# Rank products laid out in sequence, the norm's root ahead of the rank copy, and zero fills issued in steps

## The chip, the cores and the metric

The kernel runs on one core of one Trainium2 chip. The core has five engines with an instruction queue each: PE (TensorE, matmuls; its weight loads are listed as PEld), DVE (VectorE), ACT (ScalarE), POOL (GpSimd) and SP (SyncE, which here only issues DMAs). DMA engines move data between the device's main memory and the on-chip buffer. The metric is the device time of one execution, in microseconds (us). Times of before and after are medians over several executions. Profiles come from one profiled execution.

## The reference

The computation is a chain of four rounds over a graph with 3125 nodes of 256 features and 50000 edges, sorted by destination. Each round is a graph layer and a feed-forward layer with experts, both behind a layer norm and added to the nodes' features:

```python
x = x + _L0_gnn_ref(_layernorm(x), edge_weight, src, dst)      # segment_sum(w * xn[dst]) into src
x = x + _L0_ffn_ref(_layernorm(x)[None], ...)[0]               # top-2 of 8 experts
x = x + _L1_gnn_ref(_layernorm(x), edge_index, ...)            # attention, 4 heads, twice
x = x + _L1_ffn_ref(...)[0]
x = x + _L2_gnn_ref(...) ; x = x + _L2_ffn_ref(...)[0]
x = x + _L3_gnn_ref(...) ; x = x + _L3_ffn_ref(...)[0]
```

The change touches only the set-up (in which the edges are put in order on the chip) and the first graph layer, `_L0_gnn_ref`: for each edge, the normed features of one end, times the edge's weight, are added to the features of the other end.

## The kernel before

**Tiles.** The 3125 nodes lie in T = 25 blocks of P = 128 (one node per partition), each node with D = 256 features. `X` holds all nodes. The edges lie in 416 columns of 128 slots: 17 columns (KB) for each of the first 24 destination blocks, 8 (KL) for the last.

**Set-up, `look`.** It sorts and bins the edges. Near its end, `own_send(21)` issues 21 indirect DMAs from POOL (L1881), which scatter records of another graph into `os_table`. Beside them run two generators. `norm_sums` computes mean and variance of the nodes on ACT (L1338, L1343), and in its last step scales the sums (L1345), takes the root (`rsqrt`, L168, on ACT with a load of its function table; then five small DVE operations, L170 to L174) and L1347. `rank_edges` finds the rank of each edge among those of one source block:

- L1418 (DVE) makes `h`, a 0/1 mark of shape (edge column, source block) in bf16, `P x 416 x 25`, in three cuts of 204, 204 and 8 columns. L1424 (PE) counts with it.
- L1432 (DVE) fills `eqd`, 16 planes of 416 columns with equality marks. L1437 (PE) adds them with an identity matrix: 16 matmuls of 416 columns.
- L1443 (DVE) multiplies `h` with the starts of each block into `q`, again `P x 416 x 25`, cut by cut. L1448 (PE) adds the 25 unit products: matmul t reads `q[:, :, t]`, one element in 25.
- L1451 (ACT) copies the sum, the ranks, out of PE's accumulation buffer. After it stands `next(norm)`, the root.

In `look`, the instructions of DVE and of ACT keep the order in which the program writes them. Then a flag (L1329, L1330, DVE) tells whether the edges fit; `settle` (L1893) issues one DMA from SP; all engines read the flag (L2848) and branch. The rest of the work stands in `FAST_STEPS`.

**The fills, `clear`.** It is the first of these steps: 26 DMAs from SP, 1 MB each, that write zeros into `regions` (27 MB in main memory). `regions` is scattered into at the end of round one's graph layer (L872) and read by the feed-forward layer.

**Round one's graph layer, `r0_gnn`.** It first fills buckets for five destination blocks (`fill_bucket`, L1500). A bucket needs ACT for one-hot rows of ranks (L1515, L1516, 17 columns), DVE for L1519, L1523 and L1530, PE for 17 matmuls (L1526), and ACT for two copies (L1528, L1529). Then it runs through five groups g of five destination blocks, and in each through 25 source blocks: 125 steps. One step is:

- DVE compares for the source (L1600, `r_hs`) and the destination (L1605, `r_hd`, five times);
- PE multiplies them into five 128 x 128 weight blocks (L1609, `r_pw`);
- ACT copies these out (L1613, `r_wt`) into one fifth of a `wide` buffer, of which there are two; when a buffer is full, SP writes its 1.6 MB to `mats` (L1615);
- PE applies the blocks of the step before to the normed features (L1575, `r_pa`), DVE adds the result into `X` (L1576), ACT copies a column (L1577); POOL issues two sends.

While group g runs, the buckets of group g + 1 are filled, one in five steps. In the last group each step also scatters a block into `regions`. Outside `look` a scheduler sets the order of the instructions on each engine from its own estimates of durations, and an engine works in that order; SP's queue is one of them. A DMA holds one of eight semaphores ("lanes") shared by SP's and ACT's queues; the next DMA on the lane can be issued only when the one before has landed. ACT's queue also issues small loads (`gx_b`, L965) and three 1 MB zero writes (`ff_results`, L1015) during g = 0.

Of the kernel before, what the change touches and what calls it, by code (L numbers as in the profile page):

```python
# [25 lines left out]
BF16 = mybir.dt.bfloat16  # L26
# [7 lines left out]
P = 128  # L34
N = 3125
T = 25
# [15 lines left out]
KB = 17  # L52
# [11 lines left out]
class Net:  # L64
# [30 lines left out]

    def clear(self):

        v = self.regions.rearrange("(q p r) d -> q p r d", p=P, r=8)
        for q in range(v.shape[0]):
            self.nc.sync.dma_start(v[q], self.zero[:, None, 0:D].to_broadcast([P, 8, D]))  # L100

# [1114 lines left out]
class Fast(Net):  # L1218
# [171 lines left out]
    def rank_edges(self, pool, eqd, identb, both, over, norm):  # L1390


        nc, tc, s = self.nc, self.tc, self.d
        K = s.K
        with tc.tile_pool(name="re_ps", bufs=2, space=PSUM) as psp, tc.tile_pool(name="re_pr", bufs=1, space=PSUM) as psr:
            blk = pool.tile([P, K], BF16, name="re_blk")
            bi = pool.tile([P, K], I32, name="re_bi")
            nc.vector.tensor_copy(bi, s.rec[:, :, 0])
            nc.vector.tensor_scalar(bi, bi, 7, None, op0=OP.arith_shift_right)
            base = pool.tile([P, K], F32, name="re_base")  # L1400
            self.block_start(base)

            far = pool.tile([P, K], F32, name="re_far")

            place = s.rec[:, :, 1]
            nc.vector.tensor_sub(place, place, base)
            nc.vector.tensor_scalar(far, place, float(P), 64.0, op0=OP.is_ge, op1=OP.mult)
            nc.vector.tensor_tensor(blk, bi, far, OP.add)
            h = pool.tile([P, K, T], BF16, name="re_h")
            start = pool.tile([P, T, T], BF16, name="re_start")  # L1410
            top = pool.tile([P, 3], F32, name="re_top")
            cuts = ((0, 12, KB), (12, T - 1, KB), (T - 1, T, KL))
            sums = []
            last = psr.tile([P, 512], F32, name="re_r")
            for i, (u, v, kb) in enumerate(cuts):
                n = (v - u) * T
                k0, k1 = s.k0[u], s.k0[u] + (v - u) * kb
                nc.vector.tensor_tensor(h[:, k0:k1], blk[:, k0:k1, None].to_broadcast([P, k1 - k0, T]),  # L1418
                                        self.iotab[:, None, 0:T].to_broadcast([P, k1 - k0, T]), OP.is_equal)
                hv = h[:, k0:k1, :].rearrange("p (d k) s -> p k d s", k=kb)  # L1420
                ps = psp.tile([P, 2, 512], F32, name="re_p") if i < 2 else last[:, K:K + 2 * T].rearrange("p (j s) -> p j s", j=2)
                for j in range(2):
                    for k in range(kb):
                        nc.tensor.matmul(ps[:, j, 0:n].rearrange("p (d s) -> p d s", s=T), both[:, j, :], hv[:, k],  # L1424
                                         start=k == 0, stop=k == kb - 1)
                sums.append(ps)
            next(norm)

            for ks, ds, nd, kb in self.parts():
                bv = blk[:, ks].rearrange("p (d k) -> p d k", k=kb)  # L1430
                for g in range(1, kb):
                    nc.vector.tensor_tensor(eqd[:, g - 1, ks].rearrange("p (d k) -> p d k", k=kb)[:, :, g:kb],  # L1432
                                            bv[:, :, g:kb], bv[:, :, 0:kb - g], OP.is_equal)
            q = pool.tile([P, K, T], BF16, name="re_q")
            ranks = last[:, 0:K]
            for g in range(1, KB):
                nc.tensor.matmul(ranks, identb, eqd[:, g - 1, :], start=g == 1, stop=False)  # L1437
            for i, (u, v, kb) in enumerate(cuts):
                n = (v - u) * T
                k0, k1 = s.k0[u], s.k0[u] + (v - u) * kb  # L1440
                nc.vector.tensor_copy(start[:, u:v, :].rearrange("p d s -> p (d s)"), sums[i][:, 0, 0:n])
                four = [P, v - u, kb, T]
                nc.vector.tensor_tensor(q[:, k0:k1, :].rearrange("p (d k) s -> p d k s", k=kb),  # L1443
                                        h[:, k0:k1, :].rearrange("p (d k) s -> p d k s", k=kb),
                                        start[:, u:v, None, :].to_broadcast(four), OP.mult)
                nc.vector.tensor_reduce(top[:, i:i + 1], sums[i][:, 1, 0:n], AX.X, OP.max)
            for t in range(T):
                nc.tensor.matmul(ranks, identb, q[:, :, t], start=False, stop=t == T - 1)  # L1448
            nc.vector.tensor_reduce(over, top, AX.X, OP.max)
            nc.vector.tensor_scalar_add(over, over, float(-P))  # L1450
            nc.scalar.copy(s.rank, ranks)  # L1451
            next(norm)

    def block_start(self, base):

# [76 lines left out]
    def r0_gnn(self):  # L1532
# [5 lines left out]
        nc, tc, s = self.nc, self.tc, self.d  # L1538
# [3 lines left out]
        G = 5  # L1542
        self.mix_way = ExitStack()
        m = self.mix = self.mix_start(self.mix_way, "L0_ffn_Wg", ("L0_ffn_bg", "L0_ffn_bias"), 8, act=True)
        with ExitStack() as ctx:
            pool = ctx.enter_context(tc.tile_pool(name="r0", bufs=1))
# [12 lines left out]
            def norm(t):  # L1559
                nc.scalar.activation(xn[:, t, 0:D], self.X[:, t, :], AF.Identity, scale=s.rstd[:, t:t + 1],  # L1560
                                     bias=s.mean[:, t:t + 1])
# [10 lines left out]
            def apply(g, src, wt):  # L1572
                pa = psa.tile([P, D + 1], F32, name="r0_pa")
                for i in range(G):
                    nc.tensor.matmul(pa, wt[:, i, :], xn[:, g * G + i, :], start=i == 0, stop=i == G - 1)  # L1575
                nc.vector.tensor_add(self.X[:, src, :], self.X[:, src, :], pa[:, 0:D])  # L1576
                nc.scalar.copy(degs[:, src, g:g + 1], pa[:, D:D + 1])  # L1577
                if g == T // G - 1:

                    self.mix_send(m, 2)  # L1580
                    for _ in range(1 if src < T - 2 else 2):
                        self.mix_step(m, src + 1)


            for d in range(G):
                for _ in self.fill_bucket((bp, psb), f5, d):
                    pass
                self.own_send(8, self.filled)
            last = None
            for g in range(T // G):  # L1590
                ds = slice(g * G, g * G + G)
                for src in range(T):
                    if g == 0 and src + TG < T:
                        norm(src + TG)
                    if g + 1 < T // G:
                        if src % G == 0:
                            fill = self.fill_bucket((bp, psb), f5, (g + 1) * G + src // G)
                        next(fill, None)
                    hs = hp.tile([P, G, P], F32, name="r0_hs")
                    nc.vector.tensor_tensor(hs, self.iota[:, None, :].to_broadcast([P, G, P]),  # L1600
                                            s.bsrc[:, ds, src, None].to_broadcast([P, G, P]), OP.is_equal)
                    hd = hp.tile([P, G, P], F32, name="r0_hd")
                    for i in range(G):
                        d = g * G + i
                        nc.vector.tensor_scalar(hd[:, i, :], iota1, s.bdst[:, d, src:src + 1], s.bw[:, d, src:src + 1],  # L1605
                                                op0=OP.is_equal, op1=OP.mult)
                    pw = psw.tile([P, G, P], F32, name="r0_pw")
                    for i in range(G):
                        nc.tensor.matmul(pw[:, i, :], hd[:, i, :], hs[:, i, :], start=True, stop=True)  # L1609
                    if src % G == 0:  # L1610
                        wide = wp.tile([P, G, G, P], F32, name="r0_wt")
                    wt = wide[:, src % G]
                    done = nc.scalar.copy(wt, pw)  # L1613
                    if src % G == G - 1:
                        nc.sync.dma_start(self.mats[:, src - G + 1:src + 1, ds, :], wide)  # L1615
                    if last:
                        apply(*last)
                    last = (g, src, wt)
                    self.own_send(2 if g < T // G - 1 else src % 2, done)
# [1215 lines left out]
        self.own_graph.close()  # L2835


FAST_STEPS = ("clear", "r0_gnn", "take_edges", "middle", "r2_gnn", "r2_ffn", "r3_gnn", "r3_ffn")
STEPS = ("clear", "sort_src", "sort_dst", "r0_gnn", "r0_ffn", "r1_gnn", "r1_ffn", "sort_own", "r2_gnn", "r2_ffn",
         "r3_gnn", "r3_ffn")  # L2840

# [2 lines left out]
def network(ctx: ExitStack, tc: tile.TileContext, a, out):  # L2844
# [4 lines left out]
    for fast in (True, False):  # L2849
        with cmp.Else() if not fast else tc.If(fits > 0) as cmp, ExitStack() as way:  # L2850
            way_net = object.__new__(Fast if fast else Net)
            way_net.__dict__.update(net.__dict__, way=way, fast=fast)
            way_net.edges = way.enter_context(tc.tile_pool(name="edges", bufs=1))
            for step in FAST_STEPS if fast else STEPS:
                getattr(way_net, step)()
# [32 lines left out]
```

## Time and profile before

| what | value |
|---|---|
| median of 6 runs | 5660.24 us (5647.51 to 5676.73) |
| the profiled execution | 5653.63 us, span 5651.7 us |
| busy share of the span | PE 65%, DVE 49%, ACT 39%, POOL 37% |
| set-up until the flag (L1330) | 135.8 us |
| the 26 zero fills, first to last issue | 136.50 to 246.8 us |
| `r_wt` copy of step 0 and of step 24 of g = 0 | 172.33 and 324.01 us |
| the same of steps 0 and 24 of g = 1 | 327.35 and 410.28 us (3.46 a step) |

The times in the profile count from the start of the span. In a timeline a row has the start, the time, the engine, the source line, the operation with its output and inputs, the size, and how many instructions were joined into the row; in brackets stands how long the engine had been idle and what ended that: another engine's instruction, a DMA, or "issue" where the profile shows nothing that was waited for. A table by stretches has the busy time of each engine, the clock that PE was granted as a share of its full one, the busy share of the DMA engines and the rate that they moved. A list of waits has total, number and longest.

### The profile page before, as it was taken

The page shows a single profiled execution, that of the slowest core. Times are in us where ns is not written, and L with a number is a line of the kernel's source. Part 1 is how long each engine was busy: PE and PEld are TensorE (multiplying, and loading weights), DVE is VectorE, ACT ScalarE, POOL GpSimd, SP SyncE. Part 2 cuts the span into 40 slices and gives each one's busy share as a digit, 9 for nine tenths or more (in the row PEclk, how much of TensorE's full clock was granted, in tenths as well). Part 3 has the DMA queues.
Part 4 walks back from the last instruction along what each step waited for, and adds up shares of the span by engine and source line. Part 5 has one row for each costly group of instructions (what it writes and reads, how often), then busy time and mean ns, then how long its engine had stood idle before and what let it go on. Part 6 is the DMA issues. An engine that isn't in the chain of part 4 may idle for free. (4 is left out here: it accounts for less than half of the span.)

```text
span 5651.7 us, 66370 instructions
## 1 busy us (share of the span) xinstructions
PE 3678.1 (65%) x21000; PEld 2882.9 (51%) x21000; DVE 2793.5 (49%) x9308; ACT 2189.7 (39%) x6055; POOL 2107.0 (37%) x2108
## 2 busy tenths in 40 slices
PE   5499879335554324444573887554666699997994
PEld 2499768223333223333352776432333488886883
DVE  7588631534444334554525787425545788422112
ACT  4656422135454335455411897311222443112221
POOL 3566333555555455565357000245554000011003
PEclk8699979666666656666696998776777899997997
DMA  1632256333333133333162321201111011233554
GB/s 56 216 109 94 103 165 212 108 88 105 96 106 96 52 86 103 90 103 96 59 199 76 110 101 71 58 18 26 22 22 25 8 58 65 88 102 131 188 189 142
DMA packets 329539, 542.62 MB, mean 96 GB/s; under 512 B 69426, under 2 KB 242102, under 8 KB 325972
## 3 DMA queue, kind: packets, MB, share of 16 engines
q1 hardware_dynamic: 213520, 354.48, 18.7%
q0 software_dynamic: 84032, 154.27, 10.5%
q10 hardware_dynamic: 31620, 29.44, 1.6%
q8 instruction: 174, 2.85, 0.2%
q14 instruction: 193, 1.58, 0.1%
HBM read 393.09 MB, written 145.37 MB: 95 GB/s over the span
## 5 line engine op out<-in xcount | busy, mean ns | idle before, releaser
L363 POOL DMA_INDIRECT ad_rows<-r_rows,fa_gi x832 | 829.5, 997 | 621.4 <-PE ad_acc L2278 333.8
L1881 POOL DMA_INDIRECT os_table<-os_rec,os_at x512 | 544.4, 1063 | 642.8 <-ACT gx_h L1008 183.5
L363 POOL DMA_INDIRECT ad_rows<-q_rows,own_gi x416 | 400.6, 963 | 869.2 <-DVE ad_hb L2159 508.4
L2268 ACT ACTIVATE ad_rows<-ad_rows 128x64 f32<-128x64 f32 x2544 | 637.1, 335 | 121.3 <-issue 119.3
L2278 PE MATMUL ad_acc<-ad_rows,ad_hd 128*128 128x260 f32 x1664 | 596.4, 519 | 37.2 <-ACT ad_rows L2268 32.8
L2278 PEld LDWEIGHTS ad_acc<-ad_rows,ad_hd 128*128 128x128 f32 x1664 | 413.9, 263 | 126.6 <-ACT ad_rows L2268 42.2
L1710 PE MATMUL r_pa<-r_xs,r_cnt 128*128 128x257 bf16 (+1 forms) x3750 | 459.0, 276 | 11.6 <-issue 10.7
L872 POOL DMA_INDIRECT regions<-gh_xn,gd_at x150 | 148.4, 989 | 843.5 <-PE r_pa L1710 544.8
L1008 ACT ACTIVATE gx_h<-gx_pa,gx_bias 128x256 f32<-128x256 f32 x392 | 184.7, 473 | 605.9 <-PE gx_pa L1007 558.3
L1710 PEld LDWEIGHTS <-r_cnt 128*128 128x128 bf16 x3750 | 364.4, 99 | 66.2 <-issue 15.2
L1007 PE MATMUL gx_pa<-gx_xt,gx_w 128*128 128x256 f32 x1568 | 370.3, 392 | 23.7 <-DVE gx_xt L1002 21.8
L977 PE MATMUL gx_po<-gx_w,gx_h 128*128 128x256 f32 x1568 | 373.0, 384 | 9.5 <-ACT gx_h L1008 8.1
L979 DVE TENSOR_TENSOR gx_ys<-gx_po,gx_b 128x256 f32<-128x256 f32 x168 | 70.6, 423 | 567.5 <-PE gx_po L977 505.2
L1007 PEld LDWEIGHTS gx_pa<-gx_xt,gx_w 128*128 128x128 f32 x1568 | 297.6, 194 | 90.8 <-DVE gx_xt L1002 40.8
L363 POOL DMA_INDIRECT gb_y<-ff_results,gd_at x150 | 154.4, 1029 | 487.2 <-SPq L126 437.2
L1575 PE MATMUL r_pa<-r_xn,r_wt 128*128 128x257 f32 x1250 | 306.9, 391 | 35.0 <-ACT r_wt L1613 32.6
L2167 ACT CAST ad_hd<-ad_hb 128x2176 f32<-128x2176 bf16 (+1 forms) x50 | 98.3, 1967 | 581.6 <-PE ad_acc L2278 430.7
L2181 PE MATMUL ad_pt<-ident,ad_e 128*4 128x128 f32 x75 | 26.1, 348 | 452.4 <-DVE ad_e L2178 184.4
L977 PEld LDWEIGHTS gx_po<-gx_w,gx_h 128*128 128x128 f32 x1568 | 293.8, 193 | 51.7 <-ACT gx_h L1008 12.1
L2655 PE MATMUL ss_sum<-r_xw,ss_wt 128*128 128x256 f32 x1250 | 289.9, 394 | 6.3 <-DMA ss_wt<-mats 6.3
L2237 PE MATMUL ad_px<-ad_nb,ad_hT 128*128 128x24 bf16 x1248 | 45.4, 180 | 341.6 <-DVE ad_nb L1470 235.9
L1575 PEld LDWEIGHTS r_pa<-r_xn,r_wt 128*128 128x128 f32 x1250 | 233.3, 196 | 67.0 <-ACT r_wt L1613 34.4
(588 smaller groups left out, 7230.7 us busy)
## 6 DMA issues: line engine op xcount, KB each, us to landing
gx_w<-in_L_ffn_W SPq DMA_DIRECT2D x56, 1024.0 KB
mats<-r_wt SPq DMA_DIRECT2D x25, 1600.0 KB
ss_wt<-mats SPq DMA_DIRECT2D x25, 1600.0 KB
gx_w<-in_L_ffn_W SPq DMA_DIRECT2D x56, 512.0 KB
regions<-zero SPq DMA_DIRECT2D x26, 1024.0 KB
ad_rb<-fa_relT SPq DMA_DIRECT2D x48, 544.0 KB
gx_xs<-regions SPq DMA_DIRECT2D x84, 256.0 KB
ff_results<-gx_ys ACTq DMA_DIRECT2D x84, 256.0 KB
```

What stands on the lines that cost most here:

```text
L363: return self.nc.gpsimd.indirect_dma_start(out=out, out_offset=None, in_=table[:, :], in_offset=bass.IndirectOffsetOnAxis(ap=idx, axis=0))
L872: ins = nc.gpsimd.indirect_dma_start(out=self.regions[:, :], out_offset=bass.IndirectOffsetOnAxis(ap=m.at[i][:, t:t + 1], axis=0), in_=x, ...
L977: nc.tensor.matmul(po, h[:, f, j * P:(j + 1) * P], w2s[:, f, :], start=f == 0, stop=f == FC - 1)
L1007: nc.tensor.matmul(ps, w1s[:, c, f * P:(f + 1) * P], xt[:, c, :], start=c == 0, stop=c == DC - 1)
L1008: done = nc.scalar.activation(h[:, f, :], ps, act, bias=bias1[:, f, k:k + 1])
L1575: nc.tensor.matmul(pa, wt[:, i, :], xn[:, g * G + i, :], start=i == 0, stop=i == G - 1)
L1710: nc.tensor.matmul(pa[:, 0:n], c[:, u, :], xs[i][:, u, j, 0:n], start=u == 0 and j == 0, stop=u == T - 1 and j == 2)
L1881: i = nc.gpsimd.indirect_dma_start(out=s.table[:, :], out_offset=bass.IndirectOffsetOnAxis(ap=s.at[:, c:c + 1], axis=0), in_=s.rec[:, c, : ...
L2167: nc.scalar.copy(x.hd[:, :x.kb, :], x.hb[:, :x.kb, :])
L2268: i = nc.scalar.activation(v, v, AF.Copy, scale=x.rt[:, k, W4 + h:W4 + h + 1])
L2278: nc.tensor.matmul(x.acc, lhs[:, k, :], rhs[:, k, :], start=i == 0, stop=i == x.kb - 1)
L2655: nc.tensor.matmul(sums[t], wt[:, d, :], xw[:, d, :], start=d == 0, stop=d == T - 1)
```

## The change

It has three parts. In `rank_edges`, `q` is laid out with the source block outermost, so that each of PE's 25 unit products reads a contiguous row; DVE's L1443 therefore writes with its innermost step at 416 elements. The additions into the ranks are done cut by cut: 3 x (16 + 25) matmuls of 204, 204 and 8 columns instead of 16 + 25 of 416. As those of one cut stand ahead of the next cut's product, DVE's second write into `q` waits for PE's reads of the first cut.

The step that takes the norm's root moves ahead of the rank copy on ACT.

`clear` is no longer a step of its own. Its 26 fills come from a generator that `r0_gnn` asks for one fill at every fourth source block, and for the rest ahead of the last group. In SP's queue, as the scheduler then sets it, three small loads come first, then 14 fills, the first write of `mats`, four fills, the second write, four fills, the third, four fills, and then the other writes of `mats`. ACT's bucket work in g = 0 (L1515, L1516) is spread evenly among the steps; before, that of about five buckets stood in one piece ahead of step 10.

```diff
--- before.py
+++ after.py
@@ -95,9 +95,15 @@
 
     def clear(self):
 
+        for _ in self.clear_steps():
+            pass
+
+    def clear_steps(self):
+
         v = self.regions.rearrange("(q p r) d -> q p r d", p=P, r=8)
         for q in range(v.shape[0]):
             self.nc.sync.dma_start(v[q], self.zero[:, None, 0:D].to_broadcast([P, 8, D]))
+            yield
 
 
 
@@ -1431,25 +1437,25 @@
                 for g in range(1, kb):
                     nc.vector.tensor_tensor(eqd[:, g - 1, ks].rearrange("p (d k) -> p d k", k=kb)[:, :, g:kb],
                                             bv[:, :, g:kb], bv[:, :, 0:kb - g], OP.is_equal)
-            q = pool.tile([P, K, T], BF16, name="re_q")
+            q = pool.tile([P, T, K], BF16, name="re_q")
             ranks = last[:, 0:K]
-            for g in range(1, KB):
-                nc.tensor.matmul(ranks, identb, eqd[:, g - 1, :], start=g == 1, stop=False)
             for i, (u, v, kb) in enumerate(cuts):
                 n = (v - u) * T
                 k0, k1 = s.k0[u], s.k0[u] + (v - u) * kb
+                for g in range(1, KB):
+                    nc.tensor.matmul(ranks[:, k0:k1], identb, eqd[:, g - 1, k0:k1], start=g == 1, stop=False)
                 nc.vector.tensor_copy(start[:, u:v, :].rearrange("p d s -> p (d s)"), sums[i][:, 0, 0:n])
                 four = [P, v - u, kb, T]
-                nc.vector.tensor_tensor(q[:, k0:k1, :].rearrange("p (d k) s -> p d k s", k=kb),
+                nc.vector.tensor_tensor(q[:, :, k0:k1].rearrange("p s (d k) -> p d k s", k=kb),
                                         h[:, k0:k1, :].rearrange("p (d k) s -> p d k s", k=kb),
                                         start[:, u:v, None, :].to_broadcast(four), OP.mult)
                 nc.vector.tensor_reduce(top[:, i:i + 1], sums[i][:, 1, 0:n], AX.X, OP.max)
-            for t in range(T):
-                nc.tensor.matmul(ranks, identb, q[:, :, t], start=False, stop=t == T - 1)
+                for t in range(T):
+                    nc.tensor.matmul(ranks[:, k0:k1], identb, q[:, t, k0:k1], start=False, stop=t == T - 1)
             nc.vector.tensor_reduce(over, top, AX.X, OP.max)
             nc.vector.tensor_scalar_add(over, over, float(-P))
+            next(norm)
             nc.scalar.copy(s.rank, ranks)
-            next(norm)
 
     def block_start(self, base):
 
@@ -1586,10 +1592,15 @@
                 for _ in self.fill_bucket((bp, psb), f5, d):
                     pass
                 self.own_send(8, self.filled)
-            last = None
+            last, clear = None, self.clear_steps()
             for g in range(T // G):
+                if g == T // G - 1:
+                    for _ in clear:
+                        pass
                 ds = slice(g * G, g * G + G)
                 for src in range(T):
+                    if src % 4 == 0:
+                        next(clear, None)
                     if g == 0 and src + TG < T:
                         norm(src + TG)
                     if g + 1 < T // G:
@@ -2835,7 +2846,7 @@
         self.own_graph.close()
 
 
-FAST_STEPS = ("clear", "r0_gnn", "take_edges", "middle", "r2_gnn", "r2_ffn", "r3_gnn", "r3_ffn")
+FAST_STEPS = ("r0_gnn", "take_edges", "middle", "r2_gnn", "r2_ffn", "r3_gnn", "r3_ffn")
 STEPS = ("clear", "sort_src", "sort_dst", "r0_gnn", "r0_ffn", "r1_gnn", "r1_ffn", "sort_own", "r2_gnn", "r2_ffn",
          "r3_gnn", "r3_ffn")
 
```

## The prediction

> **What bounds the kernel now.** The page says little here: PE is busy 65% and the chain of what ended last covers only the final gather. So I read three stage views. First the busy time of each engine by stretch, from the end of set-up into round one (columns: stretch, its length, busy us and count for PE, PEld, DVE, ACT, POOL, then PE clock, DMA share, GB/s):
> ```profile
> core 0: us, PE busy (x) PEld busy (x) DVE busy (x) ACT busy (x) POOL busy (x), PEclk, DMA share, GB/s
> ...
> 160.00:200.00 40.00, 25.90 (x151) 21.80 (x150) 24.05 (x53) 22.90 (x67) 31.77 (x28) 0.71 1.00 316
> 200.00:240.00 40.00, 13.70 (x53) 11.54 (x54) 9.38 (x21) 11.06 (x29) 25.31 (x24) 0.60 0.49 153
> 240.00:280.00 40.00, 22.29 (x167) 18.51 (x166) 31.01 (x58) 36.11 (x108) 11.09 (x8) 0.70 0.39 136
> 280.00:320.00 40.00, 40.00 (x234) 36.31 (x233) 28.41 (x78) 18.80 (x49) 23.62 (x25) 0.96 0.40 136
> 320.00:400.00 80.00, 80.00 (x516) 73.23 (x515) 65.62 (x173) 40.48 (x115) 49.92 (x47) 1.00 0.29 104
> ```
> From 280 on PE bounds round one. Before that, in group g=0, no engine is full from 200 to 240, and ACT alone from 240 to 280. The timeline names the holes:
> ```profile
> 194.70 52.65 SPq L100 DMA_DIRECT2D regions<-zero  x6
> ...
> 222.27 0.69 ACT L1613 COPY r_wt<-r_pw 128x640 f32<-128x640 f32 x1 [25.05 <-issue]
> 222.27 0.83 DVE L1600 TENSOR_TENSOR r_hs<-iota,bu_src 128x640 f32<-128x640 f32 x1 [23.64 <-issue]
> ...
> 223.01 4.65 PE L1575 MATMUL r_pa<-r_xn,r_wt 128*128 128x257 f32 x10 [28.03 <-ACT r_wt L1613]
> ...
> 231.95 0.70 ACT L1613 COPY r_wt<-r_pw 128x640 f32<-128x640 f32 x1
> ...
> 247.47 0.69 ACT L1613 COPY r_wt<-r_pw 128x640 f32<-128x640 f32 x1
> ...
> 277.78 1.26 ACT L1613 COPY r_wt<-r_pw 128x640 f32<-128x640 f32 x2
> ```
> The r_wt copy marks a step: step 0 is at 172.33, steps 4, 5, 9 and 10 stand above, step 24 is at 324.01. Two holes: about 36 us from 186.4, where PE's instructions come 0.7 us apart and then stop, until 223.0; and 30 us from step 9 to step 10. The 26 fills hold the DMA engines at share 1.00 from 137 to 219.2. The waits of SP's queue say why the last fill, and all behind it, came later still:
> ```profile
> SPq L100 <- DMA gx_b<-in_L_ffn_b: 35.0, 1, 35.0
> ```
> The first mats write so leaves at 257.49. Third, the end of set-up in the timeline:
> ```profile
> 106.29 2.92 DVE L1443 TENSOR_TENSOR re_q<-re_h,re_start 128x5100 bf16<-128x5100 bf16 x1
> 106.43 3.62 POOL L1881 DMA_INDIRECT os_table<-os_rec,os_at  x1 [0.30 <-issue]
> ...
> 113.84 18.13 PE L1448 MATMUL re_r<-re_q,fl_ident 128*128 128x416 bf16 x25 [1.90 <-DVE re_top L1446]
> ...
> 128.12 0.97 POOL L1881 DMA_INDIRECT os_table<-os_rec,os_at  x1 [0.30 <-issue]
> ...
> 132.01 0.51 ACT L1451 CAST fa_rank<-re_r 128x416 bf16<-128x416 f32 x1 [17.27 <-PE re_r L1448]
> ```
> PE's 18.13 us lead to the rank copy, Sqrt and flag (135.64). But POOL's 21 sends end at 129.1, and round one needs POOL too (gd_base at 136.94, for which DVE's L771 waits). Each send that overlaps a big two-input DVE operation lasts as long as that operation.
>
> **Part 1, the rank products.** L1448 reads q with a hop of 25 elements: 0.72 us for 416 columns. L1437 reads 416 contiguous columns in 0.17. In three cuts, 25 × (0.09 + 0.09 + 0.03) = 5 us, most of it beside DVE's second product. So PE saves some 17 us. The writer pays: the q product L1443 now writes bf16 with a hop of 416 elements. No row shows that; call one strided product X. Lower end: 2.92, as now. Nearest rows: casts that write bf16 five elements apart, L1466 in 0.75 us per 416 (1.8 ns each, contiguous neighbours about 0.5), so X = 5100 × 1.7 = 8.7, which I take, as the hop is alone on the output. Upper end: L1470, hopping on read and write, 1.30 us per 416, 3.1 ns, X = 16. The h product L1418, without a hop but with a broadcast innermost operand, took 5.46, in between.
> The second write also waits for PE's 25 reads of cut 0. So the first product ends at 106.3 + X; some 2.7 us of PE and small DVE work follow; the second ends at 109 + 2X. Two sends are held by the products, one fits between, and 11 more at their free pitch of 1.28 end POOL at 124.2 + 2X. The flag, with Sqrt behind the last sum and no longer behind the rank copy, comes at about 114 + 2X, ahead of POOL. POOL to the first round-one work is 1.7 us: 125.9 + 2X against 137.1. D = −5.4, **+6.2**, +20.8 us for X = 2.92, 8.7, 16.
> [...]
>
> **Part 2, Sqrt ahead of the rank copy.** ACT loses nothing: the copy (0.51) moves behind table load (1.28) and Sqrt (0.23). The DVE chain no longer waits 19.04 us for ACT, but POOL covers it: 0 beyond D. With POOL's cover gone, it would be worth the 0.5.
>
> **Part 3, the fills.** No bytes are removed. In SP's new order gd_wg and the two biases go first (0.67, 1.11 and 1.17 us of SP, inside the 8 us that SP has left before mats 0), then 14 fills at once, then mats 0, four fills, mats 1, four, mats 2, four, then mats alone. SP stands at each mats until the fifth copy of its group, so what is queued behind it is four fills, for which nobody waits until the last group scatters into regions. Three 1 MB ff_results zeros on ACT's queue come at steps 12 to 14, against 253 and later. The listed orders also change ACT: before, about five buckets' L1515 and L1516 work stood ahead of step 10's copy (the 36 busy us of 240:280); now one bucket's work lies among each five steps. POOL's order stays, and past r0_gnn nothing moves.
> New g=0, from step 0 to step 24:
> - Start: 172.33 + 6.2 = 178.5.
> - Pitch. PE needs 2.34 + 1.28 less overlap = 3.29 (the pitch of steps 10 to 24) plus a bucket's 1.14 per five steps = 3.52. DVE: 0.82 + 1.40 + 0.42, and a bucket's 3.2 over five = 3.3. ACT about 3.2. Steps 0 to 3 ran at 3.6, steps 5 to 9, with a bucket among them, at (247.47 − 231.95)/4 = 3.88. I take 3.8: 24 × 3.8 = 91.2 (84.5 to 93.1).
> - DMA. 14 fills at 3.3 each (25 landed in 82.7 us) are done at about 189, before mats 0 is due near 197. Mats 0 to 2 each have at most four fills ahead or so (13 us) and their buffer is needed again 19 us after issue; with the three zeros in the third group about 4 us of slack remain. 0 on the path, 10 us if that slack fails.
> - The slow PE stretch: 36 us before, and it ended 4 us after the fills. What made it is not in the profile; a second one, 228.0 to 231.4, had no DMA beside it. Between 0 and 36 I take 15: the first 14 fills end near the point (50 us after the first) at which it began, but DMA stays busy beside the steps.
> Step 24: 178.5 + 91.2 + 15 = 284.7 against 324.0, **39 us earlier**. What is behind it (PE-bound groups, later rounds) shifts whole. [...]
> The profiled run took 5653.6 (span 5651.7); the median is 5660.2, 6.6 more. 5653.6 − 39.3 + 6.6 = **5621**. Bounds: D −5.4, no slow stretch, pitch 3.52 gain 72.6, 5588; D +20.8, 36, 3.88 gain 1.8, 5658.
>
> **Rivals.** 0.3% is 17 us, about what can be told from no change.
> - A, 0.58: as worked out, its own range 5588 to 5658.
> - B, 0.19: the slow stretch stays whole at 36 us, only the hole before step 10 goes: 178.5 + 91.2 + 36 = 305.7, gain 18, 5642. For it: DMA stays saturated much of the time. Against: PE ran at 137 to 186 with share 1.00.
> - C, 0.14, slower: PE starves whenever fills run. Before, 36.6 us were lost in 32.8 us of saturated DMA (186.4 to 219.2). After, 12 fills, 3 zeros (3.3 each) and four mats (5 each) lie beside steps, 70 us, so 78 lost: step 24 at 348, +24, 5684. It loses from 54 us on, and shows from 71. Against: 137 to 186 again, and the steps from 280 at share 0.40.
> - D, 0.09: nothing comes of it, since the fills were hidden and the bucket work, only spread, still costs what the second hole cost: pitch 6.06, within 0.3%. Against: steps 5 to 9 at 3.88.
>
> **How the numbers follow.** Faster by over 0.3% (below 5643): 0.52 of A, 0.10 of B, 0.01 of D: 0.63. Within: 0.06 of A, 0.09 of B, 0.06 of D: 0.21. Slower: C and 0.02 of D: 0.16. The range 5588 to 5672 leaves out C and the low tail of A.
>
> **What would show it.** PE's L1448 matmuls near 0.09 us each; L1443 at X; POOL's last send at 124.2 + 2X; step 0's copy at 178; fills issued in bursts of 14, 4, 4, 4; no hole over 20 us between copies; step 24 near 285; g=1 at its old 86 us. Wrong if X exceeds 20, if step copies halt while fills run, or if a copy into r_wt waits for mats.

## The result and the profile after

The changed kernel takes 5673.49 us (median of 27 runs, 5661.14 to 5681.95) against 5662.99 us before (56 runs). The ratio is 1.0019, with a 95% interval from 1.0013 to 1.0025: 10.5 us slower, where 39 us less had been forecast. The profiled execution has a span of 5669.4 us against 5651.7.

First the busy time by stretch of the changed kernel, at the hand-over from set-up to round one (columns as in the table of before: stretch, length, busy us and count of PE, PEld, DVE, ACT, POOL, then PE's granted clock, DMA share, GB/s):

```profile
core 0: us, PE busy (x) PEld busy (x) DVE busy (x) ACT busy (x) POOL busy (x), PEclk, DMA share, GB/s
160.00:200.00 40.00, 11.63 (x128) 10.00 (x126) 34.13 (x54) 27.95 (x80) 20.45 (x16) 0.50 0.75 240
200.00:240.00 40.00, 24.96 (x133) 22.25 (x134) 16.93 (x42) 17.88 (x49) 30.89 (x30) 0.76 0.65 209
240.00:280.00 40.00, 17.77 (x102) 15.46 (x103) 18.88 (x43) 16.45 (x45) 27.37 (x22) 0.66 0.25 76
280.00:320.00 40.00, 39.59 (x259) 35.89 (x259) 35.76 (x91) 26.24 (x77) 29.21 (x24) 1.00 1.01 326
320.00:400.00 80.00, 78.50 (x521) 71.08 (x520) 67.59 (x174) 51.02 (x145) 47.07 (x47) 1.00 0.35 122
```

ACT's full stretch at 240 to 280 is gone, but PE is still busy for only 17.8 of these 40 us, now with the DMA engines at 0.25. The timeline of set-up shows where the start went (line numbers are six to eleven higher than before: L1449 is the product L1443, L1454 the matmul L1448, L1892 POOL's send L1881, L1624 the `r_wt` copy L1613; "remote" in brackets stands for a release whose origin the profile does not show):

```profile
106.76 22.32 DVE L1449 TENSOR_TENSOR re_q<-re_h,re_start 128x5100 bf16<-128x5100 bf16 x1
107.01 22.44 POOL L1892 DMA_INDIRECT os_table<-os_rec,os_at  x1 [0.31 <-issue]
...
129.14 4.41 PE L1454 MATMUL re_r<-re_q,fl_ident 128*128 128x204 bf16 x25 [19.44 <-DVE re_top L1452]
...
133.58 22.28 DVE L1449 TENSOR_TENSOR re_q<-re_h,re_start 128x5100 bf16<-128x5100 bf16 x1 [4.09 <-PE re_r L1454]
134.86 21.35 POOL L1892 DMA_INDIRECT os_table<-os_rec,os_at  x1 [0.30 <-issue]
...
163.94 0.23 ACT L174 ACTIVATE rs_r<-ns_s 128x25 f32<-128x25 f32 x1 [47.42 <-DVE re_top L1452]
...
166.71 0.14 POOL L768 IOTA gd_down<- 128x8 f32 x1 [0.29 <-issue]
```

PE's 25 reads fell from 18.13 us to 4.41 for half the columns. Each of the two large products rose from 2.92 to 22.3 us, and one of POOL's sends stood still until the end of each. The flag comes 30 us later (165.81 against 135.64), the first step 31. The `r_wt` copies of steps 3, 4, 5, 6, 9 and 10 in ACT's timeline:

```profile
214.43 0.67 ACT L1624 COPY r_wt<-r_pw 128x640 f32<-128x640 f32 x1
228.75 0.69 ACT L1624 COPY r_wt<-r_pw 128x640 f32<-128x640 f32 x1 [8.14 <-remote]
262.98 0.69 ACT L1624 COPY r_wt<-r_pw 128x640 f32<-128x640 f32 x1 [9.31 <-remote]
266.51 0.67 ACT L1624 COPY r_wt<-r_pw 128x640 f32<-128x640 f32 x1
...
277.40 0.69 ACT L1624 COPY r_wt<-r_pw 128x640 f32<-128x640 f32 x1
280.68 0.70 ACT L1624 COPY r_wt<-r_pw 128x640 f32<-128x640 f32 x1
```

Steps 3 to 6 take 52.1 us (52.9 before): the slow PE stretch is there whole. Step 10 follows step 9 after 3.3 us (30.3 before): that hole is gone. Copy by copy against the kernel before:

| step of g=0 | before | after | later by |
|---|---|---|---|
| 0 | 172.33 | 203.61 | 31.3 |
| 3 | 183.07 | 214.43 | 31.4 |
| 6 | 236.01 | 266.51 | 30.5 |
| 9 | 247.47 | 277.40 | 29.9 |
| 10 | 277.78 | 280.68 | 2.9 |
| 24 | 324.01 | 332.46 | 8.4 |

So the start loses 31, the second hole gives back 27, and the steps from 10 to 24, which now have bucket work among them, cost 5.5 more. The rest of round one runs 9 to 11 us later. The profiled pair ends 17.7 apart; the other 7 or so come and go in later stages of these two executions, and the medians do not show them.

### The profile page after: what moved, and what is told of

Read it like the earlier page. It is cut to its first block, busy times and chain, and to the rows that moved or that the text cites. A ratio compares the mean times of both kernels' runs of the same rounds, so it can differ in the third digit from the quotient of the medians.

```text
span 5669.4 us, 66521 instructions
## 1 busy us (share of the span) xinstructions
PE 3663.0 (65%) x21082; PEld 2887.7 (51%) x21082; DVE 2828.9 (50%) x9308; ACT 2188.8 (39%) x6055; POOL 2152.5 (38%) x2108
## 3 DMA queue, kind: packets, MB, share of 16 engines
q0 software_dynamic: 84032, 154.27, 10.5%
## 5 line engine op out<-in xcount | busy, mean ns | idle before, releaser
L1892 POOL DMA_INDIRECT os_table<-os_rec,os_at x512 | 589.3, 1151 | 620.7 <-ACT gx_h L1014 192.0
L1013 PE MATMUL gx_pa<-gx_xt,gx_w 128*128 128x256 f32 x1568 | 374.6, 395 | 25.1 <-DVE gx_xt L1008 18.3
L2666 PEld LDWEIGHTS ss_sum<-r_xw,ss_wt 128*128 128x128 f32 x1250 | 245.6, 198 | 41.6 <-issue 6.7
```

Source lines behind the costliest of these rows:

```text
L1013: nc.tensor.matmul(ps, w1s[:, c, f * P:(f + 1) * P], xt[:, c, :], start=c == 0, stop=c == DC - 1)
L1892: i = nc.gpsimd.indirect_dma_start(out=s.table[:, :], out_offset=bass.IndirectOffsetOnAxis(ap=s.at[:, c:c + 1], axis=0), in_=s.rec[:, c, : ...
L2666: nc.tensor.matmul(sums[t], wt[:, d, :], xw[:, d, :], start=d == 0, stop=d == T - 1)
```

## The experiments

**Theory S:** two effects of opposite sign. The new layout makes DVE's product dear and delays round one by 31 us; the stepwise fills remove the hole before step 10; the slow PE stretch is touched by neither. **Rival R:** the stepwise fills themselves cost something, or fills in flight make the slow stretch, as the prediction's half-way value and its rival C held. The experiments lie in four sets, each with the kernel before measured beside them. Its time was 4816 us in the first set, 5627 in the second, 4815 in the third and 5628 in the fourth (5663 where the result was taken). Therefore each experiment is compared with the kernel before of its own set only. The record gives the sets the chip numbers 2, 12, 7 and 7: one number stands for both times, so what makes the two kinds of set differ is not known.

### The parts alone

**Part 3 alone** (e1): the kernel before with `clear_steps`, the two calls in `r0_gnn`, and `FAST_STEPS` without `"clear"`.

```diff
-            last = None
+            last, clear = None, self.clear_steps()
...
+                    if src % 4 == 0:
+                        next(clear, None)
```

> The kernel before with part 3 alone (fills in steps; q and the root's place as before). Theory S: the two parts pull against each other. Set-up is as before, so step 0 copies at 172 and no product writes with a hop; the 30 us between step 9 and step 10 shrink to a pitch of 3 to 4; the slow PE stretch of about 38 us stays. Step 24 at 324 - 23 = 301, and the time 23 us under before, 5640 (ratio 0.996). Rival R: the stepwise fills cost something too, and the q layout is not the whole loss: then less than 10 us is gained.

Measured: 4790.83 against 4816.39 us, ratio 0.9952 (0.9938 to 0.9965). That is 25.6 us gained, as S has it; R's "less than 10" falls. The absolute numbers were not as expected, since the kernel before itself took 4816 us here, and the slow stretch was absent (11.3 us from step 3 to step 6).

**Part 1 alone** (e2): the kernel before with the new `q`.

```diff
-            q = pool.tile([P, K, T], BF16, name="re_q")
+            q = pool.tile([P, T, K], BF16, name="re_q")
```

and the product and matmuls of the change's diff; the root stays behind the rank copy.

> The kernel before with part 1 alone (q in sequence; root behind the rank copy; fills first). S: two products of 22.3 us, POOL's last send near 166, step 0's copy near 204, everything behind shifted by 31 us: 5694 (ratio 1.0055). R: the set-up's delay is partly taken up later (the fills start later too, the hole before step 10 ends with them), and less than 20 us are lost.

Measured: 4845.34 against the same 4816.39, ratio 1.006 (1.0046 to 1.0073), 29.0 us lost; R's "less than 20" falls. The `r_wt` copies of its steps 3, 6, 9 and 10 read as follows:

```profile
210.54 0.69 ACT L1613 COPY r_wt<-r_pw 128x640 f32<-128x640 f32 x1
...
221.83 0.69 ACT L1613 COPY r_wt<-r_pw 128x640 f32<-128x640 f32 x1
...
232.38 0.69 ACT L1613 COPY r_wt<-r_pw 128x640 f32<-128x640 f32 x1
265.37 1.29 ACT L1613 COPY r_wt<-r_pw 128x640 f32<-128x640 f32 x2 [2.04 <-DMA mats<-r_wt]
```

Two things are seen. The hole before step 10 belongs to the kernel before and not to the kind of set: 33 us here too, the last 2 of them a wait for a `mats` write, most of the rest ACT's bucket work (ACT is busy 17.5 of the 20 us from 240 to 260). And in this set steps 3 to 6 take 11.3 us while the fills hold the DMA engines at 1.00 (210 to 222 us): there is no slow stretch.

**Part 2 alone** (e3):

```diff
-            nc.scalar.copy(s.rank, ranks)
             next(norm)
+            nc.scalar.copy(s.rank, ranks)
```

> The kernel before with part 2 alone: the root ahead of the rank copy. If POOL's sends set the end of set-up, as the prediction has it: Sqrt near 116 instead of 133.8, the flag at about 133, POOL's first work of round one unchanged at 136 or up to 0.5 earlier, time within 3 us of before. If the chain rank copy, table load, Sqrt, flag sets it: about 2 us earlier as well, no more, since the rank copy waits for the same matmuls; but gains over 5 us would refute that POOL covers.

Measured: 5622.74 against 5627.34 us, ratio 0.9992 (0.9982 to 1.0001); in the profiles step 0 comes 3.7 and step 24 4.1 us earlier than in the kernel before of the same set (b_before, below). The interval just includes no change, so the cause is read from the trace. The end of its set-up in the timeline:

```profile
119.01 0.15 DVE L1330 TENSOR_SCALAR fa_flag<-fl_f 128x1 int32<-128x1 f32 x1
...
130.23 0.17 POOL L762 IOTA gd_down<- 128x8 f32 x1
...
133.14 0.51 ACT L1452 CAST fa_rank<-re_r 128x416 bf16<-128x416 f32 x1 [15.72 <-PE re_r L1448]
```

The flag comes 16.6 us earlier than before (135.64), far ahead of the 133 that was expected, and POOL goes straight on when its sends end (130.23; 136.54 before). The rank copy alone is now last. In the kernel before, POOL had waited for the flag:

```profile
136.54 0.14 POOL L762 IOTA gd_down<- 128x8 f32 x1 [7.45 <-DVE fa_flag L1330]
```

So the root's chain did set the end of the old set-up, by some 4 us, and POOL's sends did not cover it. Neither case of the expectation is met: the gain lies above the 2 to 3 us that they allow, and below the 5 us named as the refutation.

**The kernels themselves beside them:**

> The kernel before itself, profiled beside the other experiments. It tells which of the two holes in g=0 belong to the kernel: if the scheduler's order makes the one between step 9 and step 10 (S), it is there, 30 us; the slow PE stretch was absent from the first experiments, with fills in flight (e1) and without (e6), and if it belongs to the chip and not to the fills, it is absent here too, with 26 fills in flight: step 9 near 203, step 10 near 236, step 24 near 281.

> The changed kernel itself beside the other experiments. S: set-up loses 31 us, g=0 gains 26, so it stands 4 to 5 us above before; with the 8 us by which e1 and e2 bracket it, 0 to 0.2% slower. If the two parts disturbed one another, it would differ from the sum of e1 (-25.6) and e2 (+29.0), +3.4, by more than 5 us.

Measured in the second set: the kernel before 5618.17 (one run; 5627.34 is the median of the set), with 53.2 us from step 3 to step 6 and 30.4 from step 9 to 10. The expectation that the slow stretch would be absent missed. The changed kernel took 5636.09 against 5627.34, ratio 1.0015 (1.0006 to 1.0024), with 50.4 us from step 3 to 6 and step 24 7.2 us later than in the profile of before of the same set. e1 and e2 add up to +3.4 us against +8.7 measured, with an interval from 3 to 14: the parts add, as far as can be told.

### What the hop costs

The first two experiments leave open what in the product is dear. **The hop moved to the read** (e5), in the changed kernel:

```diff
-                four = [P, v - u, kb, T]
-                nc.vector.tensor_tensor(q[:, :, k0:k1].rearrange("p s (d k) -> p d k s", k=kb),
-                                        h[:, k0:k1, :].rearrange("p (d k) s -> p d k s", k=kb),
-                                        start[:, u:v, None, :].to_broadcast(four), OP.mult)
+                four = [P, T, v - u, kb]
+                nc.vector.tensor_tensor(q[:, :, k0:k1].rearrange("p s (d k) -> p s d k", k=kb),
+                                        h[:, k0:k1, :].rearrange("p (d k) s -> p s d k", k=kb),
+                                        start[:, u:v, :].rearrange("p d s -> p s d")[:, :, :, None].to_broadcast(four), OP.mult)
```

> The changed kernel, with the product's loop turned: it writes q contiguously in the new layout and reads h with a hop of 25 elements. If the price sits on the write (S): a product takes 5.5 to 9 us (the row of before with a hop on the read alone, L1398, took 0.53 us per 416 elements, 1.3 ns), POOL's last send comes near 136 to 142, step 0 near 172 to 178, and the time is 5640 to 5646. If any hop costs alike (rival): 22 us a product and 5673, as the changed kernel.

Measured: 4797.41 against 4816.39 us, ratio 0.9959 (0.9945 to 0.9972), 19.0 us gained with the same layout of `q`. The product and the send that it holds in the timeline:

```profile
106.70 9.02 DVE L1449 TENSOR_TENSOR re_q<-re_h,re_start 128x5100 bf16<-128x5100 bf16 x1
106.95 9.58 POOL L1892 DMA_INDIRECT os_table<-os_rec,os_at  x1 [0.30 <-issue]
```

So most of the price sits on the write; with the hop on the read a product still takes 9.0 us against 2.92. With X = 9.0, the prediction's sum 125.9 + 2X gives a start 6.8 us later than before; step 0 came at 176.97, 4.6 later. The layout as such was not the whole fault, but neither does it pay here: part 3 alone gained 25.6 us in the same set, 6.6 more than this kernel with all three parts.

**Ten products in one kernel** (e7), the kernel before with these ahead of its first product:

```diff
+        for hop, t in ((204, 25), (418, 24), (416, 25), (512, 20), (424, 24), (520, 20)):
+            out = flat[:, 0:t * hop].rearrange("p (s k) -> p s k", s=t)[:, :, 0:n]
+            nc.vector.tensor_tensor(out.rearrange("p s (d k) -> p d k s", k=kb), ...)
...
+        (a product with a hop of 2 elements; a copy with hop 416; a product into 4-byte words with hop 208;
+         a product with a contiguous output that reads h with a hop of 25)
```

> The kernel before with ten more products ahead of the first one, into the same buffer, which is written over afterwards; the result is as before. They write 204 x 25 bf16 (or 24 or 20 of the 25) with a hop on the output of 204, 418, 416, 512, 424 and 520 elements, then of 2 elements, then a one-input copy with hop 416, the product as 4-byte words with a hop of 208 (the same 832 bytes), and the product with a contiguous output and the hop on the read. If the price is that of a bf16 element written alone (theory): every bf16 hop costs 4.4 ns, also 2 elements apart, and 4-byte words clearly less. If it is the distance of 832 bytes: hop 416 stands out from 418, 424, 512, and 4-byte words 832 bytes apart cost the same. If it belongs to two inputs: the copy is cheap. POOL's sends stand still for each two-input product and not for the copy.

Measured in one run (5771.66 us). The groups of DVE that write `q`, by form (busy us in all, then mean ns of one):

```profile
L1462 DVE TENSOR_TENSOR re_q<-re_h,re_start 128x5100 bf16<-128x5100 bf16 x2 | 44.3, 22137 | 0.1
L1462 DVE TENSOR_TENSOR re_q<-re_h,re_start 128x4896 bf16<-128x4896 bf16 x2 | 42.4, 21216 | 0.1
L1462 DVE TENSOR_TENSOR re_q<-re_h,re_start 128x4080 bf16<-128x4080 bf16 x2 | 36.4, 18184 | 0.1
L1468 DVE COPY re_q<-re_h 128x5100 bf16<-128x5100 bf16 x1 | 11.3, 11325 | 0.0
L1472 DVE TENSOR_TENSOR re_q<-re_h,re_start 128x5100 bf16<-128x5100 bf16 x1 | 8.9, 8934 | 0.0
L1470 DVE TENSOR_TENSOR re_q<-re_h,re_start 128x5100 f32<-128x5100 bf16 x1 | 8.7, 8719 | 0.0
L1446 DVE TENSOR_TENSOR re_q<-re_h,re_start 128x5100 bf16<-128x5100 bf16 x2 | 5.8, 2921 | 0.1
L1466 DVE TENSOR_TENSOR re_q<-re_h,re_start 128x5100 bf16<-128x5100 bf16 x1 | 5.8, 5816 | 0.0
```

Divided by the elements of one product:

| write | ns per element |
|---|---|
| contiguous bf16 (the kernel's own) | 0.57 |
| bf16, hop of 2 elements | 1.14 |
| 4-byte words, hop of 208 (832 bytes) | 1.71 |
| contiguous bf16, hop of 25 on the read, `start` repeated along the innermost step | 1.75 |
| one-input copy, bf16, hop of 416 | 2.22 |
| bf16, hop of 204 and 416 elements | 4.34 |
| bf16, hop of 418 and 424 | 4.33 |
| bf16, hop of 512 and 520 | 4.46 |

No distance stands out between 204 and 520 elements, so it is not the 832 bytes. Words of four bytes with the same byte distance cost 1.71, two-byte elements 4.34. But "written alone" is not the whole of it either, as the theory had it: two elements apart costs only 1.14. The copy costs half of the product. Why two-byte elements far apart are the dear case is not shown. POOL's sends stood still for the one-input copy too, where the expectation had them move: one took 16.69 us, across the product with hop 2 and the whole copy (235.95 to 247.27).

```profile
230.71 16.69 POOL L1903 DMA_INDIRECT os_table<-os_rec,os_at  x1 [0.30 <-issue]
```

### The slow PE stretch and the fills

**No fill in g=0** (e6), the fills held behind copies of groups 1 and 2:

```diff
+                    if g in (1, 2) and src % 2 == 0:
+                        self.fill_after = done
+                        next(clear, None)
```

with each fill made to wait for `fill_after`; and **64 idle PE matmuls** (e8) at the head of round one in the kernel before:

```diff
+            for _ in range(64):
+                nc.tensor.matmul(idle[:, 0:P], self.iotab, self.iotab, start=True, stop=True)
```

> The kernel before, with all 26 fills held until groups g=1 and g=2, each behind that step's copy, so that none is in flight in g=0. If the slow PE stretch (0.7 us and more between PE's instructions, steps 3 to 6) has nothing to do with the fills (S): it stays at about 38 us with a DMA share under 0.3 beside it, the hole before step 10 goes, step 24 at 300, and the time is 5640. If the fills make it (the prediction's rival C and half of its forecast): it goes, step 24 near 263, 5602.

Measured: 4795.57 against 4816.39 us, ratio 0.9959 (0.9946 to 0.9973), 4.7 us less gain than part 3 alone, with overlapping intervals; steps 3 to 6 take 11.3 us with (e1) and 11.2 without fills beside them. Of the slow stretch this run decides nothing, since its set had none. The third set had none either:

> e1 again, to meet a chip on which the slow PE stretch appears (it did beside b_before and not beside e1). If such a chip is met, S: the stretch costs 41 us between step 3 and step 6, as in before (52.9 us against 11.3 without it), the hole before step 10 is gone, step 24 at 324 - 24 = 300, and the time is 20 to 26 us under before. On a chip without it: as e1, ratio 0.995.

> e6 again, for the same reason: no fill in flight in g=0. On a chip with the slow stretch, S: the 41 us stay with a DMA share under 0.3 between step 3 and step 6, the time equals that of the stepwise fills within 5 us. If fills make the stretch on such a chip: it shrinks under 15 us and the time lies 25 us or more under the stepwise fills.

> The kernel before with 64 idle PE matmuls of 0.06 us (128 PE instructions with their weight loads) at the head of round one, where PE waits anyway. If the slow stretch belongs to a count of PE's instructions since the branch: it comes 128 instructions, 2.7 steps, earlier, before step 3. If it belongs to the time or to what the other engines do at that point: it stays between steps 3 and 6. On a chip without the stretch it tells nothing but that the matmuls are hidden.

Measured against 4814.96 us: stepwise fills 4791.64 (0.9955, 0.9942 to 0.9969), late fills 4793.27 (0.9952, 0.9939 to 0.9966), idle matmuls 4813.0 (one run). The fourth set has the stretch:

> Part 3 alone once more, for a chip with the slow PE stretch. S: there as well 20 to 26 us under before (ratio 0.9955), with 50 to 53 us from step 3 to step 6. If the fills beside the steps make the stretch longer on such a chip: under 10 us are gained.

> No fill in flight in g=0, for a chip with the slow PE stretch. S: from step 3 to step 6 50 to 53 us as in before, with a DMA share under 0.3; time within 5 us of part 3 alone. If the fills make the stretch: 11 to 25 us there, and 25 us or more under part 3 alone.

> 64 idle PE matmuls (128 PE instructions) ahead of round one, for a chip with the slow PE stretch. If it belongs to a count of PE's instructions since the branch, it comes 2.7 steps earlier, before step 3; if not, it stays between steps 3 and 6.

Measured against 5628.44 us: stepwise fills 5600.87 (0.9951, 0.9938 to 0.9964), late fills 5601.58 (0.9954, 0.9941 to 0.9966), idle matmuls 5615.44 (one run). From step 3 to step 6 they took 51.1, 52.3 and 53.3 us. The busy times of the late fills (e6c), in the set that has the stretch:

```profile
core 0: us, PE busy (x) PEld busy (x) DVE busy (x) ACT busy (x) POOL busy (x), PEclk, DMA share, GB/s
160.00:200.00 40.00, 28.14 (x170) 24.73 (x167) 26.32 (x60) 26.14 (x75) 31.77 (x28) 0.79 0.13 42
200.00:220.00 20.00, 5.31 (x16) 4.33 (x17) 2.00 (x5) 2.97 (x7) 15.13 (x17) 0.61 0.02 0
220.00:240.00 20.00, 7.48 (x27) 5.93 (x27) 7.93 (x18) 7.52 (x21) 11.44 (x10) 0.54 0.01 1
240.00:260.00 20.00, 20.00 (x141) 18.20 (x140) 20.00 (x49) 14.15 (x39) 16.69 (x11) 1.00 0.56 189
```

and of the stepwise fills (e1) in a set that has not:

```profile
160.00:200.00 40.00, 34.52 (x224) 30.95 (x222) 37.84 (x86) 38.28 (x110) 32.99 (x24) 0.84 0.96 311
200.00:220.00 20.00, 20.00 (x147) 18.38 (x146) 20.00 (x49) 13.38 (x40) 16.65 (x12) 1.00 1.01 327
```

In the first, PE is busy for 5.3 and 7.5 of 20 us with the DMA engines idle (0.02 and 0.01); in the second, PE is full with them at 1.01. Fills in flight are neither needed for the slow stretch nor enough for it. 128 more PE instructions ahead of it did not move it to an earlier step. In e7, whose set-up is 159 us longer, it stands between steps 3 and 6 as well (52.0 us), so it keeps to a place in the program and not to a time. It goes with the kind of set: every profile of the sets at 5627 and 5628 has it, none of those at 4815 and 4816. What makes it stays open. PE's granted clock falls with it (0.61 and 0.54, against 1.00 in the other set), but the clock is also 0.50 where PE merely has little to do (11.63 of 40 us in the changed kernel, 160 to 200), so cause and consequence are not told apart.

### Without the new layout

**Parts 2 and 3** (e9), the kernel before with the fills in steps and the root ahead of the rank copy:

> The kernel before with parts 2 and 3, without the new layout of q. The gains add up: 20 to 26 us from the fills, 4 to 5 from the root ahead of the rank copy (e3), so 25 to 30 us under before, ratio 0.994 to 0.9955, and 3 to 6 us under the fills alone in the same call. If the start of round one is then held by something else (POOL's sends end at 129.3 + 1), under 2 us more than the fills alone.

> Parts 2 and 3 without the new layout, for a chip with the slow PE stretch: the gains of 20 to 26 us and of 4 to 5 us add up, ratio 0.9945 to 0.996.

Measured: 4785.33 against 4814.96 (ratio 0.994, 0.9927 to 0.9954), 29.6 us gained, 6.3 more than the fills alone in the same set; and 5595.68 against 5628.44 (0.9945, 0.9933 to 0.9957), 32.8 us gained. Both gains add up in both kinds of set. It beats both kernels: the change without its first part.

## Why the prediction was wrong, step by step

- **Part 1, "X = 5100 × 1.7 = 8.7, which I take, as the hop is alone on the output. Upper end: … X = 16": wrong.** Measured: 22.3 us, outside both ends. The nearest rows were casts with a hop of 10 bytes and of one input (L1466 hops on its read too; L1469, with a contiguous input, took the same 0.75 us); e7 shows that price grows with the distance (1.14 ns two elements apart, 4.34 at 204 and more) and is half as large for a one-input copy (2.22). The upper end came from a row that hops on both sides, but also by few bytes. Shown by e2, e5 and e7. The size of the element counts too: e7's 4-byte words, 832 bytes apart, took 1.71 ns, and two-byte elements at the same distance 2.5 times that (4.34).
- **The sum around X came out within 3 us, in part by luck.** 125.9 + 2X gives 170.5 for X = 22.3; DVE's copy of `gd_base` started at 168.38. POOL's last send ended at 166.41, against 124.2 + 2X = 168.8. Two errors partly cancel: 4.5 us and not 2.7 lie between the two products, and four sends fit there and not one. PE's matmuls took 0.18 us each and not 0.09, at a granted clock of 0.50, and those of the first cut are not hidden: DVE waited 4.09 us for them. All of L1448's matmuls together fell from 18.13 to 9.63 us, so 8.5 were saved and not 17.
- **Part 2, "POOL covers it: 0 beyond D": right for the changed kernel, wrong for the part by itself.** In the changed kernel POOL's last send ends at 166.41, after the flag (165.81); e2, which leaves the root behind the rank copy, has step 0 no later (202.91 against 203.61). In the kernel before, POOL's sends ended at 129.1 and POOL waited for the flag at 135.64. There the part is worth some 4 us (e3; 5 to 6 in the times of e9 and e9c) and not the 0.5 that the prediction gave it without POOL's cover: the root was freed of PE's whole sum and not of the copy alone.
- **Part 3, the hole before step 10: right.** 30.3 us became 3.3; part 3 alone is worth 23 to 28 us in three comparisons (e1, e1b, e1c). Taking the fills away from g=0 altogether (e6, e6b, e6c) gains 21 to 27, so it is not the stepwise issue that counts, but that they no longer stand ahead of `mats` in SP's queue and that ACT's order is another. In the trace of before the hole itself is ACT's order: ACT is busy for 27.0 of the 29.6 us between the copies of steps 9 and 10, and step 10's copy waited for no `mats` write (in e2 for 2.0 us). What a change of one without the other would bring was not run: the scheduler changes both at once.
- **The pitch, 3.8: right within 4%.** From step 0 to 24 the changed kernel took 128.9 us; less the 41 of the slow stretch that is 3.66 a step.
- **"Between 0 and 36 I take 15": wrong, 41.** The slow pieces of before together cost 52.9 − 11.3 = 41 us between steps 3 and 6 (11.3 is taken from the sets without the stretch), and the changed kernel pays the same. That the stretch ended 4 us after the fills was a coincidence. The prediction had the row that spoke against it, a second slow piece from 228.0 to 231.4 with no DMA beside it, and gave it too little weight.
- **The sum again:** 284.7 + 25.1 (start) + 26 (slow stretch) − 3.4 (pitch) = 332.4; step 24 came at 332.46. The pitch here is what is left over, so that the sum closes proves nothing. Neither large error alone would have turned the sign of this sum: with the start alone wrong 14 us of the 39 would be left, with the slow stretch alone 13. Both together make step 24 some 12 us late, 8 with the pitch.
- Of the rivals, B had the stretch right and the start wrong. C had a loss, by a mechanism that e6c and e1 refute. D had a time near no change, but by a second hole that would stay, and it went. None named the write as the thing that could turn the sign, though the text's own bound asked for it: it put the point at which X decides among the things that would make it wrong ("if X exceeds 20"), and gave that no chance.

## What to carry to other kernels

Before a layout is turned so that the reader gains, price the writer at the hop that it will really have, in bytes and element size: here 8.5 us of PE, of which POOL's sends left some 3 to be gained (e3: 130.2 against 133.1), were bought with 39 us of DVE, and with POOL's queue that stood still behind it (one send took 22.44 us, one 21.35). Turning the loop so that the write is contiguous and the read hops kept the layout at 9 us instead of 22 a product; that still gained less (19.0 us) than leaving the layout alone (29.6, e9). When no row shows an operation at its real distance, the bound is open upward; and a hole that lies next to a transfer in time is not caused by it until a case without the transfer has been looked at.

## What the hardware showed unexpectedly

- A bf16 product written with a hop of 408 to 1040 bytes takes 4.3 to 4.5 ns an element, 7.6 to 7.8 times the contiguous one (0.57); 4-byte words 832 bytes apart take 1.71, a hop of 50 bytes on the read, with the other input repeated along the innermost step, 1.75 (e7).
- A send on POOL lasted through a one-input bf16 copy with a hop on DVE as well as through a two-input product (16.69 us across both in e7).
- The same kernel takes 4815 us in some sets of runs and 5628 in others, steadily within a set. Of these 813 us, 41 lie in one stretch of round one, in which PE starts few instructions (15 matmuls in the 32.8 us from 186.4 in the kernel before) and its granted clock is lower (0.58 there, 0.61 and 0.54 in e6c), between steps 3 and 6 in every profile of such a set; in the other sets PE is busy throughout these steps (in e2, whose steps 3 to 6 lie at 210.54 to 221.83, for 20.00 and 19.85 of 20 us from 200 to 240). The cause was not found, nor whether the rest of the 813 us is of the same kind.
